# Attention's last loop: the diagonal square of scores computed as ten blocks and six TensorE transposes of finished exponentials

## The chip, the core and the metric

The kernel runs on one NeuronCore of a Trainium2 chip, in one launch. The engines are called as in the profile: PE (TensorE: matmuls and transposes; PEld is its weight load), DVE (VectorE), ACT (ScalarE), POOL (GpSimd) and SP (SyncE, which only issues DMAs). The metric is the device time of the whole kernel in microseconds, lower is better; a kernel's time is the median of its runs.

## The reference, cut to what matters

The input `x` is four images of 64 x 64 tokens with 128 channels. A first layer is a state-space block (three scans per image). A second layer is attention followed by a small feed-forward part and a mixture of experts. The change lies in the attention, which has 16 heads of 8 channels over the 4096 tokens of an image (the shape comes from `x`, not from the constants in the setup):

```python
heads = x.reshape(Bs, Ss, H, D)
qkv = _qz_ring(heads + rx_theta)            # cosines and running products
q = jnp.transpose(qkv, (0, 2, 1, 3))
scores = jnp.einsum('bhsd,bhtd->bhst', q, q) / np.sqrt(D)
attn = jax.nn.softmax(scores, axis=-1)
ctx = jnp.einsum('bhst,bhtd->bhsd', attn, q)
```

Queries, keys and values are the same tensor `q`. So the scores of token s with token t are those of t with s, and so are their exponentials: the matrix of exponentials is symmetric. The kernel doesn't subtract a maximum; it sums the exponentials through an extra column of ones in the values and divides afterwards.

## The kernel before

The program goes through the four images. A fill stage makes the inputs of the scans, then `Attention.loop` runs once per image (three times with the scans of the next image beside it, a fourth time alone with the closing work of the third and fourth images beside it), and an end stage finishes the last tokens and the experts. The fourth call, `block.loop(nb - 1, ...)`, is "the last loop" here.

**Turns and rounds.** A call of `loop` does 32 *turns*: four groups `j` of four heads by eight blocks `qb` of 512 queries. In the last loop they are sorted by query block (`by_block`), so that the tokens of a block are finished early and their closing work can run beside later turns. A turn has 32 *rounds*, one for each tile `kc` of 128 keys (`NT` is 32). Each round does three things for four heads `k`:

- `scores(i)`: four PE matmuls (line 998, `s<-qm,key`), each with 32 rows of one head's split keys (a high and a low part), giving keys on 128 partitions by 512 queries; two heads share one PSUM tile `s` of two banks (pool `ps_s`, three such tiles). Then ACT takes the exponential of each PSUM tile into an SBUF tile `e` of 1024 columns (line 1003; pool `exps`, four tiles).
- `values(i)`: four matmuls (line 1012, `acc<-e,val`) that multiply the four heads' exponentials with their values (32 columns of weights each) and add into four 32-partition strips of one PSUM tile `acc` (`ps_o`, one tile). In fp32 each matmul is two instructions, so the profile counts eight.
- `beside(i)`: a step or two of the closing work of other tokens, between the scores and the values in program order.

**What sets the order.** The stage is written under `tc.manual_schedule()`, so each engine runs its instructions in the order of the Python code. For round `i` this is: scores of round `i + 1`, then the work beside, then the values of round `i`. PE is thus one round of scores ahead. `sums` (line 1021) copies `acc` out on DVE in the last loop and leaves five POOL DMAs (lines 1027 and 1030) for three rounds later.

**Keys and queries.** Every fourth round `fetch` brings the chunk of 512 keys three chunks ahead (lines 968 and 980: `key<-d_q`, `val<-d_v`, SP's queue; ten buffers each). `masked` loads a turn's 512 queries twelve rounds ahead.

**The work beside.** `Pace.turn(share, free)` adds `share` to a credit each round and runs steps while there is credit; a step that begins with PE work only runs where `free` is true. Here the share is 1.5, and `free` is `i % 3 > 0 or i > 830`. The steps are lines 1098 to 1215: L1115 (`co`), L1138 (`zt`), L1156 (`h`), L1169 (`fo`), L1193 (`xT`), L1207 (`lg`) on PE, with small DVE steps after each; and L1342 and L1353 of the experts. In the end stage L1384, L1394 and L1407 are the experts' matmuls and transposes; L1394 are four 128x128 transposes, and L1407 are products on four strips of 32 partitions with 128 moving columns.

Of the kernel before, what the change touches and what calls it, by code (L numbers as in the profile page):

```python
# [11 lines left out]
F32 = mybir.dt.float32  # L12
AF = mybir.ActivationFunctionType
# [3 lines left out]
P = 128  # L17
C = 128
L = 4096
NT = L // P  # L20
# [11 lines left out]
H, D, FFN = 16, 8, 512  # L32
VW = 9
VJ = 60
QB = 512
F32R = mybir.dt.float32r
# [74 lines left out]
def turned(nc, a, turns, bias=None):  # L111


    if bias:
        nc.scalar.activation(turns, a, AF.Identity, scale=1.0 / (2.0 * math.pi), bias=bias[0])
        nc.scalar.activation(turns, turns, AF.Identity, bias=bias[1])
    else:
        nc.vector.tensor_scalar(turns, a, 1.0 / (2.0 * math.pi), ROUND, ALU.mult, ALU.add)
        nc.vector.tensor_scalar_sub(turns, turns, ROUND)
    nc.vector.scalar_tensor_tensor(a, turns, -TWO_PI_HI, a, ALU.mult, ALU.add)  # L120
    nc.vector.scalar_tensor_tensor(a, turns, -TWO_PI_LO, a, ALU.mult, ALU.add)
    if bias:
# [591 lines left out]
class Attention:  # L714
# [62 lines left out]
    def begin(self, loop):  # L777

        tc = self.tc
        self.pieces_of(loop, 2)  # L780
        self.big = loop.enter_context(tc.tile_pool(name="a_big", bufs=1))
        self.mid = loop.enter_context(tc.tile_pool(name="a_mid", bufs=2))
        self.exps = loop.enter_context(tc.tile_pool(name="a_exps", bufs=4))
        self.ps_s = loop.enter_context(tc.tile_pool(name="a_ps_s", bufs=3, space=PSUM))
        self.ps_o = loop.enter_context(tc.tile_pool(name="a_ps_o", bufs=1, space=PSUM))

# [158 lines left out]
            if x % 3 == 2:  # L945
                yield

    def loop(self, b, beside, by_block=False):
# [10 lines left out]
        rounds = [(j, qb, kc) for j, qb in turns for kc in range(NT)]  # L959
        queries, keys, weights, es, accs, later = {}, {}, {}, {}, {}, {}  # L960
        chunks = [(j, g) for j, _ in turns for g in range(NT // 4)]
        held = {}

        def halves(to, j, cut, first):


            src = self.q[b].rearrange("(k j) x d t -> j k (x d) t", j=4)[j]
            nc.sync.dma_start(out=to, in_=src[:, first * D : (first + 4) * D, cut])

        def fetch(at):  # L970

            if at >= len(chunks):
                return
            j, g = chunks[at]
            if held.get(g) != j:
                held[g] = j
                keys[g] = self.big.tile([P, QB], F32, tag="keys", bufs=10, name=f"key_{b}_{at}")
                halves(keys[g], j, slice(g * QB, (g + 1) * QB), 0)
                weights[g] = self.big.tile([P, 4, VJ], F32, tag="values", bufs=10, name=f"val_{b}_{at}")
                nc.sync.dma_start(out=weights[g], in_=self.v[b][:, j, g * 4 : g * 4 + 4, :])  # L980
            keys[f"{at}"], weights[f"{at}"] = keys[g], weights[g]

        def masked(j, qb):
            t = self.mid.tile([P, QB], F32, tag="qm", name=f"qm_{b}_{j}_{qb}")
            halves(t, j, slice(qb * QB, (qb + 1) * QB), 2)
            queries[j, qb] = t

        def scores(i):

            j, qb, kc = rounds[i]  # L990
            es[i] = []
            cut = slice(kc % 4 * P, kc % 4 * P + P)
            for pair in range(2):
                s_ps = self.ps_s.tile([P, 2, QB], F32, tag="s", name=f"s_{b}_{i}_{pair}")
                for k in range(2):
                    at = 32 * (2 * pair + k)
                    rows = slice(at, at + 32)
                    nc.tensor.matmul(  # L998
                        s_ps[:, k, :], keys[f"{i // 4}"][rows, cut].bitcast(F32R), queries[j, qb][rows, :].bitcast(F32R),
                        start=True, stop=True,  # L1000
                    )
                e = self.exps.tile([P, 2, QB], F32, tag="e", name=f"e_{b}_{i}_{pair}")
                nc.scalar.activation(e, s_ps, AF.Exp, scale=1.0 / math.sqrt(D))  # L1003
                es[i].append(e)

        def values(i):
            j, qb, kc = rounds[i]
            if kc == 0:
                accs[j, qb] = self.ps_o.tile([P, QB], F32, tag="acc", name=f"acc_{b}_{j}_{qb}")
            v = weights[f"{i // 4}"][:, kc % 4, :]  # L1010
            for k in range(4):
                nc.tensor.matmul(  # L1012
                    accs[j, qb][32 * k : 32 * k + 32, :], v[:, k * VW : k * VW + 32],
                    es[i][k // 2][:, k % 2, :], start=(kc == 0), stop=(kc == NT - 1),
                )
            del es[i]

        def sums(j, qb, i):

            av = self.mid.tile([P, QB], F32, tag="av", name=f"av_{b}_{j}_{qb}")  # L1020
            (nc.vector.tensor_copy if by_block else nc.scalar.copy)(av, accs.pop((j, qb)))  # L1021
            cut = slice(qb * QB, (qb + 1) * QB)

            def store():
                for k in range(4):
                    h = 4 * k + j
                    nc.gpsimd.dma_start(  # L1027
                        out=self.context[b][h * D : h * D + D, cut], in_=av[32 * k : 32 * k + D, :]
                    )
                nc.gpsimd.dma_start(  # L1030
                    out=self.total[b][qb].rearrange("(k j) t -> j k t", j=4)[j], in_=av[D::32, :]
                )
                if by_block and j == 3:
                    self.whole[b] = qb + 1

            later[i + 3] = store

        masked(0, 0)
        for at in range(3):
            fetch(at)  # L1040
        scores(0)
        for i, (j, qb, kc) in enumerate(rounds):
            if i % 4 == 0:
                fetch(i // 4 + 3)
            if i + 1 < len(rounds):
                scores(i + 1)
            if kc == NT - 12 and i + 12 < len(rounds):
                masked(*rounds[i + 12][:2])
            if i in later:
                later.pop(i)()  # L1050
            beside(i)
            values(i)
            if kc == NT - 1:
                sums(j, qb, i)
        for i in sorted(later):
            later[i]()
        self.whole[b] = L // QB
# [464 lines left out]
def tile_kernel(tc, ctx, x, in_proj_w, dirs, out_proj_w, attn, gate, weight1, weight2, out):  # L1522


    nc = tc.nc
    nb = x.shape[0]
# [30 lines left out]
    block = Attention(tc, ctx, attn, gate, cols, ident, bank, dram, t1, w_out, scans, inputs.sz, x)  # L1557
# [10 lines left out]
    block.bank = bank  # L1568
    loop = ExitStack()
    block.begin(loop)  # L1570
    scans.extra = loop.enter_context(tc.tile_pool(name="s_extra", bufs=1))
    with tc.manual_schedule():
        last = Pace()
        n = 3 * NC * NB
        for b in range(nb - 1):
# [24 lines left out]
            last = Pace(block.after(b))  # L1600
# [6 lines left out]
    blocks = L // QB  # L1607
    pairs = [(b, b + 1) for b in range(0, nb - 2, 2)] + [(nb - 2,), (nb - 1,)]
    with tc.manual_schedule():
        last = Pace(  # L1610
            last.parts, experts.biases(),
            *(
                part for images in pairs[:-1]
                for part in (experts.search(images, blocks), experts.choice(images, blocks), experts.gather(images))
            ),
            block.after(nb - 1, range(0, 4)), block.after(nb - 1, range(4, 6)), block.after(nb - 1, range(6, blocks - 1)),
            experts.search(pairs[-1], blocks - 1),
        )
        block.loop(nb - 1, lambda i: last.turn(1.5, i % 3 > 0 or i > 830), True)
        last.rest()  # L1620
        block.cut = False
    loop.close()
# [49 lines left out]
```

## Time and profile before

| | us |
|---|---|
| median of 3 runs (11411.24 to 11415.38) | 11413.67 |
| the profiled execution | 11412.32 |
| its span, first to last instruction | 11410.5 |
| last loop, 9126 to 11162 | 2036 |
| ACT busy in the last loop | 1925.4 |
| DVE busy in the last loop | 393.7 |
| L1003, exp of 128x1024 in the last loop, x2048 | 1904.7 |
| mean granted TensorE clock of the run, and in the last loop | 0.942, 0.98 |

How to read it: the span is the profiled execution's own, and 1.8 us lie around it. The busy time of an engine is the union of its instructions; matmuls are pipelined and their ends modelled, so a PE that looks busy isn't at its peak. A wait is put down to the semaphore that came last. In a timeline an ACT line with a start 0.92 us after the one before it is a back-to-back exponential: one of them lasts about 1.06 us, and the next starts before it is over.

### The profile page before, as it was taken

Reading aid. Unit: us, or ns where it says so; the run is one execution under the profiler, and the core shown is the slowest. Engines: PE = TensorE matmul, PEld = TensorE weight load, DVE = VectorE, ACT = ScalarE, POOL = GpSimd, SP = SyncE. Lnnn points to the kernel's source line nnn. Section 1 sums busy time; section 2 is a strip of 40 time slices with the busy share of each in tenths; the row PEclk is TensorE's granted clock in tenths of the full one; section 3 lists DMA queues with packets and bytes.
Section 4 is the critical chain, followed back from the end, with each engine's and each line's share of the span. In section 5 each row is a group of like instructions: output and inputs, shape, how many; then the busy total and the mean of one; then the engine's idle time right before and its main releaser. Section 6 shows DMA issues by size and latency. Waiting matters only on the chain.

```text
span 11410.5 us, 183033 instructions
## 1 busy us (share of the span) xinstructions
PE 9874.3 (87%) x68358; PEld 3273.6 (29%) x68358; DVE 8258.3 (72%) x8405; ACT 9993.7 (88%) x10828; POOL 3790.3 (33%) x3891
## 2 busy tenths in 40 slices
PE   6687792788998889899998899999998999999995
PEld 2233331222222222222222222222222223333323
DVE  6889997888888987999988979988998321111212
ACT  4566672899999999999999999999999999989992
POOL 4777784332323223424333124243331110000000
PEclk8798895899999999999999999999999999999997
DMA  6778897656565665665656755656556332222225
GB/s 188 226 231 230 226 249 198 161 145 156 142 155 155 178 174 146 158 154 142 151 147 160 194 157 156 156 141 151 146 147 162 116 100 72 76 71 84 75 65 186
DMA packets 900980, 1747.52 MB, mean 153 GB/s; under 512 B 203150, under 2 KB 443846, under 8 KB 899830
## 3 DMA queue, kind: packets, MB, share of 16 engines
q1 hardware_dynamic: 764734, 1469.68, 47.9%
q0 software_dynamic: 93856, 156.41, 4.8%
q10 hardware_dynamic: 41496, 109.71, 3.6%
q8 instruction: 537, 8.80, 0.3%
q14 instruction: 357, 2.92, 0.1%
HBM read 1379.76 MB, written 355.47 MB: 152 GB/s over the span
## 4 chain that ended last, share of the span: by engine, by line
PE 38%; ACT 24%; issue 14%; DVE 11%; DMA 10%; POOL 1%; SPq 1%; ACTq 0%; DVEq 0%; POOLq 0%
PE acc L1012 21%; ACT e L1003 20%; PE s L998 10%; DVE h L561 5%; DMA delta<-d_delta 4%; PE cv L412 2%; DMA du<-d_du 2%; DVE dB L551 1%; ACT dA L542 1%; PE y L599 1%; ACT delta L542 1%; PE fo L1169 1%; PE xd L426 1%; PE h L1156 1%; DMA w<-in_L_ffn_weight_dram 1%
## 5 line engine op out<-in xcount | busy, mean ns | idle before, releaser
L1003 ACT ACTIVATE e<-s 128x1024 f32<-128x1024 f32 x8192 | 7778.1, 1105 | 234.2 <-PE s L998 222.2
L1012 PE MATMUL acc<-e,val 128*32 128x512 f32 x32768 | 5250.2, 615 | 106.5 <-ACT av L1021 93.7
L998 PE MATMUL s<-qm,key 32*128 32x512 f32 x16384 | 2650.8, 501 | 588.8 <-ACT e L1003 558.9
L998 PEld LDWEIGHTS s<-qm,key 32*128 32x128 f32 x16384 | 1013.4, 184 | 4444.4 <-issue 2483.9
L563 POOL COPY ends<-h 128x1 f32<-128x1 f32 x1152 | 1333.8, 1159 | 2362.4 <-DVE h L561 2353.2
L551 DVE TENSOR_TENSOR dB<-du,B 128x1024 f32<-128x1024 f32 x960 | 1213.6, 1264 | 441.2 <-PE y L599 217.2
L1012 PEld LDWEIGHTS acc<-e,val 128*32 128x32 f32 x32768 | 973.5, 109 | 1608.4 <-issue 789.0
L561 DVE TENSOR_TENSOR_SCAN h<-dA,ends,dB 128x1024 f32<-128x1024 f32 x576 | 1351.2, 2346 | 110.3 <-ACT dA L542 66.2
L542 ACT ACTIVATE dA<-delta,A 128x1024 f32<-128x1024 f32 x768 | 935.7, 1218 | 500.5 <-DMA delta<-d_delta 460.8
L561 DVE TENSOR_TENSOR_SCAN h<-delta,ends,du 128x1024 f32<-128x1024 f32 x432 | 1013.2, 2345 | 127.2 <-ACT delta L542 64.3
L568 POOL TENSOR_TENSOR hC<-h,C 128x1024 f32<-128x1024 f32 x384 | 993.5, 2588 | 153.3 <-PE y L599 83.7
L542 ACT ACTIVATE delta<-delta,A 128x1024 f32<-128x1024 f32 x768 | 937.4, 1221 | 7.3 <-DVE dB L551 2.2
L572 DVE TENSOR_TENSOR du<-h,C 128x1024 f32<-128x1024 f32 x576 | 702.2, 1219 | 0.1
L572 DVE TENSOR_TENSOR dB<-h,C 128x1024 f32<-128x1024 f32 x576 | 702.2, 1219 | 0.0
L551 DVE TENSOR_TENSOR du<-du,B 128x1024 f32<-128x1024 f32 x576 | 691.6, 1201 | 5.8 <-DMA B<-d_bc 5.8
L1027 POOL DMA_DIRECT2D d_ctx<-av x512 | 260.3, 518 | 1026.1 <-DVE av L1021 647.6
L412 PE MATMUL cv<-xn,conv 128*128 128x512 f32 x1024 | 469.7, 612 | 26.8 <-DVE xn L346 17.2
L593 POOL DMA_DIRECT2D d_du<-x_delta x272 | 157.2, 578 | 1003.0 <-DVE x_delta L592 945.1
L561 DVE TENSOR_TENSOR_SCAN h<-dA,dB 128x1024 f32<-128x1024 f32 x192 | 438.9, 2286 | 50.3 <-ACT dA L542 40.9
L599 PE MATMUL y<-hC,sel 128*32 128x256 f32 x3072 | 247.8, 456 | 171.7 <-DVE o L615 160.0
L599 PE MATMUL y<-dB,sel 128*32 128x256 f32 x4608 | 378.8, 401 | 9.9 <-DVE xT L1196 4.8
L561 DVE TENSOR_TENSOR_SCAN h<-delta,du 128x1024 f32<-128x1024 f32 x144 | 329.1, 2285 | 68.3 <-issue 35.0
(246 smaller groups left out, 7200.5 us busy)
## 6 DMA issues: line engine op xcount, KB each, us to landing
delta<-d_delta SPq DMA_DIRECT2D x768, 512.0 KB
du<-d_du SPq DMA_DIRECT2D x576, 512.0 KB
du<-d_du ACTq DMA_DIRECT2D x192, 512.0 KB
key<-d_q SPq DMA_DIRECT2D x352, 256.0 KB
d_u<-u SPq DMA_DIRECT2D x48, 1024.0 KB
d_delta<-r SPq DMA_DIRECT2D x48, 1024.0 KB
B<-d_bc SPq DMA_DIRECT2D x96, 512.0 KB
C<-d_bc SPq DMA_DIRECT2D x96, 512.0 KB
```

What stands on the lines that cost most here:

```text
L412: nc.tensor.matmul(banks[2 * m + g], w["conv"][:, k, m * P : (m + 1) * P], reads(k, g), start=(k == 0), stop=(k == 3))
L542: nc.scalar.activation(tiles["delta", s], t, AF.Exp, scale=A)
L551: nc.vector.tensor_mul(tiles["du", s], du, spread[order, c, "B", j % 2])
L561: nc.vector.tensor_tensor_scan(h, dA, dB, first, ALU.mult, ALU.add)
L563: nc.gpsimd.tensor_copy(ends[order, c][:, at : at + 1], h[:, T - 1 :])
L568: nc.gpsimd.tensor_mul(tiles["du", s], h, spread[order, c, "C", j % 2])
L572: nc.vector.tensor_mul(dB, h, spread[order, c, "C", j % 2])
L599: nc.tensor.matmul(y[32 * g : 32 * g + 32, : T // 4], self.sel[:, j // 2, :], hC[:, 256 * g : 256 * g + 256], start=(j == 0), stop=(j == 3),)
L998: nc.tensor.matmul(s_ps[:, k, :], keys[f"{i // 4}"][rows, cut].bitcast(F32R), queries[j, qb][rows, :].bitcast(F32R), start=True, stop=True,)
L1003: nc.scalar.activation(e, s_ps, AF.Exp, scale=1.0 / math.sqrt(D))
L1012: nc.tensor.matmul(accs[j, qb][32 * k : 32 * k + 32, :], v[:, k * VW : k * VW + 32], es[i][k // 2][:, k % 2, :], start=(kc == 0), stop=(kc ...
L1027: nc.gpsimd.dma_start(out=self.context[b][h * D : h * D + D, cut], in_=av[32 * k : 32 * k + D, :])
```

## The change

In the last loop only (`mirror=True`), the 512 keys that are the same tokens as a turn's 512 queries are treated apart. That square has sixteen blocks of 128 by 128 per head. Of these the ten on and above the diagonal are computed and exponentiated as before; the other six are transposes of finished blocks:

- The own chunk comes first in a turn and gives three rounds for four: *top* (key tile 0, all 512 queries), *odd* (key tile 1 with queries 128 to 511, and key tile 3 with queries 384 to 511, side by side in one tile of 512) and *even* (key tile 2 with queries 256 to 511, half a tile). Top is the turn's first round, odd its eleventh, even its twenty-first; a turn has 31 rounds.
- After the values of such a round, `turned` transposes the blocks right of the diagonal on PE (four per block, one per head) into a PSUM tile from the pool of the scores, and DVE copies them to an SBUF tile `m` (one buffer). Top turns blocks (0,1) and (0,2) at once and (0,3) in the next round, so its exponentials are kept longer; odd turns (1,2) and (1,3); even turns (2,3).
- One round later, right after the next scores and ahead of the work beside, `added` multiplies each turned block with the values of its key tile into 128 columns of `acc` (four matmuls per block).
- The pool of exponentials has five tiles for four, `av` one buffer for two. The share of the work beside is 1.55, and PE steps are free after round 804.

The diff, cut to its core (renamed indices, which leave the other loops as they were, are left out):

```diff
-        self.exps = loop.enter_context(tc.tile_pool(name="a_exps", bufs=4))
+        self.exps = loop.enter_context(tc.tile_pool(name="a_exps", bufs=5))
...
+        for j, qb in turns:
+            order = [qb] + [g for g in range(NT // 4) if g != qb] if mirror else range(NT // 4)
+            base = len(chunks)
+            chunks += [(j, g) for g in order]
+            turn = [(j, qb, base + x // 4, x % 4) for x in range(NT)]
+            if mirror:
+                own, turn = [(j, qb, base, kind) for kind in ("top", "odd", "even")], turn[4:]
+                turn = own[:1] + turn[:9] + own[1:2] + turn[9:18] + own[2:] + turn[18:]
+            rounds += turn
...
                 for k in range(2):
+                    if kind == "odd":
+                        product(s_ps[:, k, :384], at, 1, 2 * pair + k, slice(128, 512))
+                        product(s_ps[:, k, 384:], at, 3, 2 * pair + k, slice(384, 512))
+                    elif kind == "even":
+                        product(s_ps[:, k, :256], at, 2, 2 * pair + k, slice(256, 512))
+                    else:
+                        product(s_ps[:, k, :], at, 0 if kind == "top" else kind, 2 * pair + k, slice(0, 512))
...
+                wide = slice(0, 256 if kind == "even" else 512)
+                nc.scalar.activation(e[:, :, wide], s_ps[:, :, wide], AF.Exp, scale=1.0 / math.sqrt(D))
...
         def values(i):
...
+            if kind == "top":
+                turned(i, [(0, 1), (0, 2)])
+                mirrors.append((i, [(0, 3)]))
+            elif kind == "odd":
+                turned(i, [(1, 2), (1, 3)])
+            elif kind == "even":
+                turned(i, [(2, 3)])
...
+        def turned(i, blocks):
+            j, qb, at, _ = rounds[i]
+            n = len(blocks)
+            ps = self.ps_s.tile([P, 2, QB], F32, tag="s", name=f"t_{b}_{i}_{blocks[0][1]}")
+            for x, (r, c) in enumerate(blocks):
+                for k in range(4):
+                    nc.tensor.transpose(ps[:, x, k * P : k * P + P], block_of(i, r, c, k), self.ident)
+            m = self.mid.tile([P, 2, 4, P], F32, tag="mirror", bufs=1, name=f"m_{b}_{i}_{blocks[0][1]}")
+            nc.vector.tensor_copy(m[:, :n].rearrange("p x k t -> p x (k t)"), ps[:, :n])
+
+            def added():
+                for x, (r, c) in enumerate(blocks):
+                    for k in range(4):
+                        add(j, qb, at, c, k, slice(r * P, r * P + P), m[:, x, k, :])
+
+            waiting.append(added)
...
             if i + 1 < len(rounds):
                 scores(i + 1)
...
+            while waiting:
+                waiting.pop()()
+            for of, blocks in mirrors:
+                turned(of, blocks)
+                del es[of]
+            mirrors.clear()
             beside(i)
             values(i)
...
-        block.loop(nb - 1, lambda i: last.turn(1.5, i % 3 > 0 or i > 830), True)
+        block.loop(nb - 1, lambda i: last.turn(1.55, i % 3 > 0 or i > 804), True, True)
```

More of the change, by code (lines that the diff above doesn't have):

```diff
@@ L946, in rings, with loop @@
                 yield
-    def loop(self, b, beside, by_block=False):
+    def loop(self, b, beside, by_block=False, mirror=False):
         nc = self.nc
@@ L958, in loop @@
             turns.sort(key=lambda turn: turn[1])
-        rounds = [(j, qb, kc) for j, qb in turns for kc in range(NT)]
         queries, keys, weights, es, accs, later = {}, {}, {}, {}, {}, {}
-        chunks = [(j, g) for j, _ in turns for g in range(NT // 4)]
-        held = {}
+        rounds, chunks, held, mirrors = [], [], {}, []
+        for j, qb in turns:
[7 more added lines that the diff above has]
+            rounds += turn
+        per = len(rounds) // len(turns)
         def halves(to, j, cut, first):
@@ L986, in masked, with product @@
             queries[j, qb] = t
+        def product(to, at, kind, k, cut):
+            rows = slice(32 * k, 32 * k + 32)
+            key = keys[f"{at}"][rows, kind * P : kind * P + P]
+            nc.tensor.matmul(
+                to, key.bitcast(F32R), queries[rounds[self.at][:2]][rows, cut].bitcast(F32R), start=True, stop=True,
+            )
         def scores(i):
-            j, qb, kc = rounds[i]
-            es[i] = []
-            cut = slice(kc % 4 * P, kc % 4 * P + P)
+            j, qb, at, kind = rounds[i]
+            self.at, es[i] = i, []
             for pair in range(2):
@@ L995, in scores @@
                 for k in range(2):
[L996 to L1001, printed above, removed]
+                    if kind == "odd":
[5 more added lines that the diff above has]
+                        product(s_ps[:, k, :], at, 0 if kind == "top" else kind, 2 * pair + k, slice(0, 512))
@@ L1002, in scores, with add @@
                 e = self.exps.tile([P, 2, QB], F32, tag="e", name=f"e_{b}_{i}_{pair}")
-                nc.scalar.activation(e, s_ps, AF.Exp, scale=1.0 / math.sqrt(D))
+                wide = slice(0, 256 if kind == "even" else 512)
+                nc.scalar.activation(e[:, :, wide], s_ps[:, :, wide], AF.Exp, scale=1.0 / math.sqrt(D))
                 es[i].append(e)
+        def add(j, qb, at, kc, k, cut, e, start=False, stop=False):
+            v = weights[f"{at}"][:, kc, :]
+            nc.tensor.matmul(
+                accs[j, qb][32 * k : 32 * k + 32, cut], v[:, k * VW : k * VW + 32], e, start=start, stop=stop,
+            )
@@ L1006, in values @@
         def values(i):
-            j, qb, kc = rounds[i]
-            if kc == 0:
+            j, qb, at, kind = rounds[i]
+            if i % per == 0:
                 accs[j, qb] = self.ps_o.tile([P, QB], F32, tag="acc", name=f"acc_{b}_{j}_{qb}")
-            v = weights[f"{i // 4}"][:, kc % 4, :]
             for k in range(4):
[L1012 to L1015, printed above, removed]
@@ L1016, in values @@
-            del es[i]
+                if kind == "even":
+                    add(j, qb, at, 2, k, slice(256, 512), es[i][k // 2][:, k % 2, :256])
+                elif kind == "odd":
+                    add(j, qb, at, 1, k, slice(128, 512), es[i][k // 2][:, k % 2, :384])
+                else:
+                    kc = 0 if kind == "top" else kind
+                    add(j, qb, at, kc, k, slice(0, 512), es[i][k // 2][:, k % 2, :], i % per == 0, i % per == per - 1)
+            if kind == "odd":
+                for k in range(4):
+                    add(j, qb, at, 3, k, slice(384, 512), es[i][k // 2][:, k % 2, 384:])
@@ new lines, in values, with block_of @@
+            if kind == "top":
+                turned(i, [(0, 1), (0, 2)])
+                mirrors.append((i, [(0, 3)]))
+            elif kind == "odd":
+                turned(i, [(1, 2), (1, 3)])
+            elif kind == "even":
+                turned(i, [(2, 3)])
+            if i not in (m[0] for m in mirrors):
+                del es[i]
+        def block_of(i, r, c, k):
+            return es[i][k // 2][:, k % 2, (c - r) * P : (c - r) * P + P]
+        def turned(i, blocks):
[9 more added lines that the diff above has]
+                for x, (r, c) in enumerate(blocks):
+                    for k in range(4):
+                        add(j, qb, at, c, k, slice(r * P, r * P + P), m[:, x, k, :])
+            waiting.append(added)
@@ L1018, in sums @@
+        waiting = []
         def sums(j, qb, i):
-            av = self.mid.tile([P, QB], F32, tag="av", name=f"av_{b}_{j}_{qb}")
+            av = self.mid.tile([P, QB], F32, tag="av", bufs=1, name=f"av_{b}_{j}_{qb}")
             (nc.vector.tensor_copy if by_block else nc.scalar.copy)(av, accs.pop((j, qb)))
@@ L1036, in sums @@
             later[i + 3] = store
-        masked(0, 0)
+        masked(*turns[0])
         for at in range(3):
@@ L1041, in loop @@
         scores(0)
-        for i, (j, qb, kc) in enumerate(rounds):
-            if i % 4 == 0:
-                fetch(i // 4 + 3)
+        seen = -1
+        for i, (j, qb, at, kind) in enumerate(rounds):
+            if at > seen:
+                seen = at
+                fetch(at + 3)
             if i + 1 < len(rounds):
                 scores(i + 1)
-            if kc == NT - 12 and i + 12 < len(rounds):
+            if i % per == per - 12 and i + 12 < len(rounds):
                 masked(*rounds[i + 12][:2])
@@ L1050, in loop @@
                 later.pop(i)()
+            while waiting:
[4 more added lines that the diff above has]
+            mirrors.clear()
             beside(i)
             values(i)
-            if kc == NT - 1:
+            if i % per == per - 1:
                 sums(j, qb, i)
```

## The prediction

> **What bounds the kernel now.** I read the stages first, then who waits for whom in the last loop, then single rounds. The change touches the last loop alone, from 9126 us (the last copy of the loop before it, L1021 on ACT) to 11162 us. Stages; after the stage come length, then busy us (xinstructions) of PE, PEld, DVE, ACT and POOL, then clock:
>
> ```profile
> core 0: us, PE busy (x) PEld busy (x) DVE busy (x) ACT busy (x) POOL busy (x), PEclk, DMA share, GB/s
> 9126.00:11162.00 2036.00, 1964.26 (x13696) 631.71 (x13692) 393.68 (x996) 1925.36 (x2079) 177.06 (x314) 0.98 0.26 76
> 9400.00:9800.00 400.00, 397.27 (x429) 1.00 0.23 69
> ```
>
> The second row is L1003 (exp) alone: 429 exps in 400 us where little else runs. So ACT holds the loop, and PE looks as full only because its overlapping ends are modelled. DVE has 1642 us free. The waits of the same stretch (total us, times, longest):
>
> ```profile
> PEld acc L1012 <- ACT e L1003: 123.1, 424, 0.8
> ACT e L1003 <- PE s L998: 99.1, 82, 7.5
> PEld acc L1012 <- DVE av L1021: 19.7, 25, 3.5
> ```
>
> The two engines wait for each other: PE for an exp 424 times, ACT for scores 82 times. One undisturbed round from the timeline (start, duration):
>
> ```profile
> 9932.37 1.11 ACT L1003 ACTIVATE e<-s 128x1024 f32<-128x1024 f32 x1
> 9932.69 0.51 PE L998 MATMUL s<-qm,key 32*128 32x512 f32 x4
> 9933.13 0.14 PEld L1012 LDWEIGHTS acc<-e,val 128*32 128x32 f32 x4 [0.25 <-issue]
> 9933.29 1.12 ACT L1003 ACTIVATE e<-s 128x1024 f32<-128x1024 f32 x1
> 9933.54 0.14 PEld L1012 LDWEIGHTS acc<-e,val 128*32 128x32 f32 x4 [0.27 <-ACT e L1003]
> 9934.52 0.51 PE L998 MATMUL s<-qm,key 32*128 32x512 f32 x4
> 9935.12 2.03 ACT L1003 ACTIVATE e<-s 128x1024 f32<-128x1024 f32 x2
> ```
>
> Scores 9932.69 to 9933.13 (0.43 us); the first two heads' values; then the other two wait until the exp of 9932.37 is done (9933.54); they end at 9934.52, where the next scores start. The round is 1.83 us. Those scores are used 0.60 us later by the exp of 9935.12, exactly when ACT is ready. Where four L1169 matmuls stood ahead of the values, scores started at 9902.95 and their exp at 9903.54, again 0.6 us, after ACT had waited. So the order is tight: PE can take in some 0.40 us between scores and values (values without a wait take 0.99, here 1.40), and whatever comes **after** the values delays ACT at once. ACT's delay is never made good, since it has no faster pace than 0.915 us an exp.
>
> **What the Trainium skill says.** *ScalarE: Activation LUTs*, section "What ACT_TABLE_LOAD costs": an ACTIVATE with immediate scale costs 186 ns + 0.833 ns an element, neighbours overlapping by 93 ns. For 1024 that is 1039; the loop's mean is 1061 and its spacing 915, so the trace agrees. For 512 elements I estimate a spacing of 0.915 - 0.427 = 0.49 us. *TensorEngine Tiling (Array Packing)*, "Key Properties": changing the tiling mode drains the engine. Transposes (128x128) lie between values (128x32) and scores (32x128), so they change it twice; the rows below contain such changes. *VectorE: DVE Perf Modes*, "Why PSUM operands drop a tier": fp32 from PSUM goes at one element a cycle. The trace agrees (0.266 us for 256 more, below). *TensorE: Matmul & The Clock Gate*, Part 2, step 1: matmuls stay in program order. So a matmul that waits for DVE holds all behind it; the third wait row above shows one.
>
> **The change, part by part**, for one of 32 turns. Prices (PE from start to the next start):
>
> ```profile
> 9929.46 0.44 PE L1193 MATMUL xT<-ident,x1r 128*128 128x128 f32 x2
> 9929.83 1.10 PE L1012 MATMUL acc<-e,val 128*32 128x512 f32 x8
> ...
> 11294.29 0.66 PE L1394 MATMUL hT<-ident,hr 128*128 128x128 f32 x4 [0.76 <-ACT hr L1389]
> 11294.88 1.06 PE L1384 MATMUL h<-w,pooled 128*32 128x512 f32 x8
> ...
> 11299.64 1.08 PE L1407 MATMUL o<-w,hs 128*32 128x128 f32 x32 [1.51 <-ACT hs L1402]
> 11300.54 1.04 PE L1384 MATMUL h<-w,pooled 128*32 128x512 f32 x8
> ```
> ```profile
> 9935.44 0.69 DVE L1196 COPY xT<-xT 128x512 f32<-128x512 f32 x1
> L1348 DVE COPY wT<-wt 128x256 f32<-128x256 f32 x24 | 10.2, 425 | 83.1 <-PE wt L1342 83.1
> ```
>
> Two transposes 0.37, four 0.59, so 0.11 each past the first: eight cost 1.03. L1407 has the very form of the mirrored products (four column groups, 128 columns, two instructions each): 0.90/32 = 28 ns, so 16 instructions cost 0.45 and 8 cost 0.22. Copies: 512 columns 0.69; 1024 columns 0.69 + 2 x 0.266 = 1.22.
>
> *Removed:* a turn has 31 rounds for 32, -1.83 us. Two of its exps are half as wide.
>
> *Top round* (blocks 1 and 2 turned after its values, block 3 one round later). Time 0 is the start of the next round's scores; undisturbed, later scores start at 1.83, 3.66, 5.49. Values end at 1.83, eight transposes take them to 2.86: scores 1.03 late. They end at 3.29. The mirrored products stand next in PE's order and wait for DVE: the last transpose ends 0.07 after the next start and DVE starts 0.11 later (as L1394 and its reader do), so 2.86 + 0.18 + 1.22 + 0.05 = 4.31. PE stands 1.02 us; behind it are block 3's transposes, the next values and scores, and for those ACT. Products to 4.76, four transposes to 5.35, values 0.99 to 6.34: the second scores are 6.34 - 3.66 = **2.68 late**. The order of the built program shows that second pair waiting for block 3's copy: 5.35 + 0.18 + 0.69 + 0.05 = 6.27, in time. The last 8 products (0.22) then fit: scores at 7.98 + 0.60 = 8.58, ACT is ready at 8.78.
>
> *Odd round* (two blocks): the same without block 3: 4.76 + 0.99 = 5.75, **2.09 late**. Its scores are eight matmuls, two after each other on one row group, 512 columns together; no row has that. Between 0 (full overlap) and 0.7 (none, 1.1 for 0.43); I take **0.30**.
>
> *Even round* (one block): the round before it ends with its own wait, so the two short exps (0.49 each) gain nothing. Its values take 0.49, four transposes 0.59: scores could start at 0.43 + 0.49 + 0.59 = 1.51, but the turned block has taken one of three score buffers, so the second pair waits for the next round's second exp: 0.60 + 0.92 + 1.11 = 2.63. Then 0.43, products 0.22, values 0.99: 4.27 for 3.66, **0.61 late**.
>
> Sum: 2.68 + 2.09 + 0.30 + 0.61 - 1.83 = +3.85 us a turn, x32 = **+123 us**. This holds where ACT bounds. Where the work beside makes PE bound, PE's own sum counts: transposes 2 x 1.03 + 2 x 0.59 = 3.24, products 1.35, two waits 2.04, less 1.5 rounds' values 1.49 and scores 0.65, plus 0.5 for the odd scores: +5.0 us, x32 = 160. The copies also queue behind other DVE work: the 25 waits for av took 19.7 us where 0.69 + 0.1 - 0.43 = 0.36 each would be 9, so some 0.25 us more; two exposed copies a turn: +16 us. I take 123 + 16 = 139.
>
> At nothing: the extra DVE time (4 copies, 3.8 us a turn, into 51 us free), the longer life of the first key chunk (its buffer of ten is not refilled until after the last use), one av buffer for two (stores end three rounds on), a fifth exp buffer. That buffer doesn't free ACT: no ACT wait for values is in the list. The pace 1.55 x 992 rounds gives 1538 steps, 1.5 x 1024 gave 1536, so the work beside ends with the loop as before; if not, its rest runs bare behind it. No DMA is added.
>
> **Sum.** Profiled execution 11412.3 us (span 11410.5 plus 1.8; median of the runs 1.4 higher) + 139 = **11551 us**.
>
> **The rivals.** (B) *Faster:* the turning hides and only the exps saved show. 32 x (2 whole exps x 0.915 + 2 x 0.427) = 86 us, giving 11326. For it: ACT is 94.6% busy in the loop and DVE mostly idle. It decides once the four disturbances cost under 1.83 us a turn in all, for which PE would need slack after values; the 0.60 us hand-over speaks against it. (C) *DVE's queue:* copies stand behind DVE instructions that wait for a DMA or for POOL (longest wait for av 3.5 us). With 1.5 us more on 64 exposed copies: 11551 + 96 = 11647. (D) Disturbances of half the size, 2.84 - 1.83 = 1.0 a turn: +32 us, 11445; and if a little less, no change.
>
> **How the numbers follow.** 0.2% is 23 us, about what a measurement of this kernel can tell from no change. Forecast 72%, own range 11490 to 11625 (odd scores 0 to 0.7: -10 to +13; PE-bound throughout +37; copies never waited for, 2 x 1.02 x 32: -65). B 14%; C 10%; D 4%, counted as same. So faster 0.14, same 0.04, slower 0.82. The range 11440 to 11650 takes in the forecast and most of C and D and leaves out B.
>
> **What would show it.** The last loop lasts 2175 us for 2036; exps of it 1920 whole and 64 half-wide; a new wait of PE for the mirror's copy, about 1 us, 64 times or more; ACT's wait for scores up from 99 us to some 300; eight transposes near 1.03, 16 products near 0.45. Wrong if that wait is short, or if scores after a turning start as before.

## The result and the profile after

| | us |
|---|---|
| after, median of 4 runs (11537.13 to 11555.27) | 11543.56 |
| before, median of 4 runs (11411.24 to 11422.50) | 11414.52 |
| ratio, 95% interval | 1.0113 (1.0096 to 1.0131) |
| after, the profiled execution (the longest of the four), and its span | 11555.27, 11553.6 |

The change makes the kernel 129 us slower by the medians; the two profiled executions, read below, lie 143 us apart. In the code of after, scores are line 999, exponentials L1019, values and mirrored products both L1024 (told apart by `acc<-e` and `acc<-m`), transposes L1062 and their copies L1064.

The last loop and the rest behind it, busy time by stage as in the table of before:

```profile
9121.00:11307.00 2186.00, 2045.92 (x16004) 749.20 (x16000) 512.97 (x1124) 1857.12 (x2015) 177.90 (x314) 0.97 0.24 71
11307.00:11553.00 246.00, 120.94 (x1156) 90.10 (x1156) 73.78 (x154) 30.61 (x49) 25.78 (x47) 0.67 0.63 216
```

The loop grew from 2036 to about 2185 us, and everything else stayed (246 us behind it; 248.5 before). ACT's busy time fell by 68 us in a loop 149 us longer: ACT now has 329 us free where it had 111. The groups of the loop, each form by itself (count, then busy us and mean ns, then idle of the engine ahead of them):

```profile
L1019 ACT ACTIVATE e<-s 128x1024 f32<-128x1024 f32 x1917 | 1801.8, 1047 | 324.4 <-PE s L999 287.4 <-PE t L1062 29.5
L1019 ACT ACTIVATE e<-s 128x512 f32<-128x512 f32 x64 | 36.4, 652 | 1.7 <-PE s L999 1.7
L1064 DVE COPY m<-t 128x1024 f32<-128x1024 f32 x64 | 78.3, 1223 | 276.8 <-PE t L1062 276.7
L1064 DVE COPY m<-t 128x512 f32<-128x512 f32 x64 | 44.2, 691 | 182.7 <-PE t L1062 182.7
```

And who waits for whom (total us, times, longest):

```profile
ACT e L1019 <- PE s L999: 289.1, 260, 9.0
PE acc L1024 <- DVE m L1064: 72.6, 68, 6.9
PEld acc L1024 <- ACT e L1019: 91.9, 309, 0.8
```

ACT's wait for scores went from 99 to 289 us, and there is a new wait of PE for the mirror's copy: 72.6 us in 68, 52 of them of 0.88 or 0.89 us. PE waits for exponentials less often (309 times for 424), since it now comes late by itself. The DVE instructions that were added cost 122 us, but DVE is idle for three quarters of the loop; only their latency counts. One top round with little work beside it, on PE:

```profile
9465.17 0.51 PE L999 MATMUL s<-qm,key 32*128 32x512 f32 x4
9465.50 0.59 PE L1221 MATMUL h<-zT,w 8*128 8x256 f32 x2
9466.05 1.07 PE L1024 MATMUL acc<-e,val 128*32 128x512 f32 x8
9467.05 1.09 PE L1062 MATMUL t<-ident,e 128*128 128x128 f32 x8
9468.07 0.51 PE L999 MATMUL s<-qm,key 32*128 32x512 f32 x4
9469.46 0.65 PE L1024 MATMUL acc<-m,val 128*32 128x128 f32 x16 [0.88 <-DVE m L1064]
9470.03 0.66 PE L1062 MATMUL t<-ident,e 128*128 128x128 f32 x4
9470.62 1.07 PE L1024 MATMUL acc<-e,val 128*32 128x512 f32 x8
9471.62 0.51 PE L999 MATMUL s<-qm,key 32*128 32x512 f32 x4
```

Eight transposes take 1.02 us (9467.05 to 9468.07). Scores end 0.43 after that, at 9468.50, and PE then stands until 9469.46, 0.96 us, for the copy; it takes 0.57 for 16 products, 0.59 for four transposes, 1.00 for values. From the scores of 9465.17 to those of 9471.62 it is 6.45 us where three undisturbed rounds less one are 3.66: 2.79 late. ACT shows the same three delays (start, length, idle before):

```profile
9449.10 18.68 ACT L1019 ACTIVATE e<-s 128x1024 f32<-128x1024 f32 x20 [1.24 <-PE s L999]
9468.67 1.02 ACT L1019 ACTIVATE e<-s 128x1024 f32<-128x1024 f32 x1 [0.90 <-PE s L999]
9470.57 1.03 ACT L1019 ACTIVATE e<-s 128x1024 f32<-128x1024 f32 x1 [0.87 <-PE t L1062]
9472.22 3.77 ACT L1019 ACTIVATE e<-s 128x1024 f32<-128x1024 f32 x4 [0.62 <-PE s L999]
```

Back-to-back exponentials overlap by about 0.13 us here, so each idle time is that much more of delay; counted from start to start, less the usual 0.915, the three are 1.03 + 0.99 + 0.74 = 2.76 us. The exponential of 9470.57 is put down to the transposes "t": it writes into the tile that top's exponentials hold for their third block. That adds nothing: it is over before 9471.62, when the scores of the next exponential (9472.22) only start. The last two delays are one wait for these scores, cut in two.

### The profile page after: what moved, and what is told of

It reads as the page before. It is cut to its first block, busy times and chain, and to the rows that moved or that the text cites. A ratio compares the mean times of both kernels' runs of the same rounds, so it can differ in the third digit from the quotient of the medians.

```text
span 11553.6 us, 187418 instructions
## 1 busy us (share of the span) xinstructions
PE 9957.7 (86%) x70662; PEld 3388.9 (29%) x70662; DVE 8380.8 (73%) x8533; ACT 9925.0 (86%) x10764; POOL 3759.2 (33%) x3891
## 4 chain that ended last, share of the span: by engine, by line
PE 36%; ACT 25%; issue 14%; DVE 14%; DMA 10%; SPq 1%; POOL 1%; ACTq 0%; DVEq 0%; POOLq 0%
ACT e L1019 21%; PE acc L1024 20%; PE s L999 9%; DVE h L561 6%; DMA delta<-d_delta 4%; PE cv L412 2%; DVE dB L551 2%; DMA du<-d_du 2%; ACT delta L542 1%; ACT dA L542 1%; PE t L1062 1%; PE fo L1234 1%; DVE m L1064 1%; PE y L599 1%; PE h L1221 1%
## 5 line engine op out<-in xcount | busy, mean ns | idle before, releaser
L1019 ACT ACTIVATE e<-s 128x1024 f32<-128x1024 f32 (+1 forms) x8128 | 7709.8, 1099 | 453.0 <-PE s L999 387.9
L1024 PE MATMUL acc<-e,val 128*32 128x512 f32 x32768 | 5156.3, 611 | 104.2 <-ACT av L1078 94.6
L563 POOL COPY ends<-h 128x1 f32<-128x1 f32 x1152 | 1298.8, 1128 | 2376.1 <-DVE h L561 2355.3
L1024 PEld LDWEIGHTS acc<-e,val 128*32 128x32 f32 x32768 | 961.6, 109 | 1558.2 <-issue 769.1
L1064 DVE COPY m<-t 128x1024 f32<-128x1024 f32 (+1 forms) x128 | 122.5, 957 | 459.5 <-PE t L1062 459.4
```

The lines of the kernel that those rows point to most:

```text
L563: nc.gpsimd.tensor_copy(ends[order, c][:, at : at + 1], h[:, T - 1 :])
L1019: nc.scalar.activation(e[:, :, wide], s_ps[:, :, wide], AF.Exp, scale=1.0 / math.sqrt(D))
L1024: nc.tensor.matmul(accs[j, qb][32 * k : 32 * k + 32, cut], v[:, k * VW : k * VW + 32], e, start=start, stop=stop,)
```

## The experiments

All ratios are to the kernel before, measured together with each run, with their 95% interval; "cost" is the difference of the two medians.

**e1_buffers.** Kernel before, with the diff's loop code but no turning, and the buffers that it uses:

```diff
-        self.exps = loop.enter_context(tc.tile_pool(name="a_exps", bufs=4))
+        self.exps = loop.enter_context(tc.tile_pool(name="a_exps", bufs=5))
...
-                keys[g] = self.big.tile([P, QB], F32, tag="keys", bufs=10, name=f"key_{b}_{at}")
+                keys[g] = self.big.tile([P, QB], F32, tag="keys", bufs=9, name=f"key_{b}_{at}")
...
-            av = self.mid.tile([P, QB], F32, tag="av", name=f"av_{b}_{j}_{qb}")
+            av = self.mid.tile([P, QB], F32, tag="av", bufs=1, name=f"av_{b}_{j}_{qb}")
```

> The kernel before with only the edits around the turning: five exponential tiles for four, one av buffer for two, and nine key and value buffers for ten (which e4 needs), no turning, the old pace. Theory (all of the loss comes from what the turning puts behind values and ahead of values on PE): 11414, within 10 us of before. Rival (the tighter or larger buffers cost something themselves): over 11425.

Measured: 11407.92 us for 11407.14, ratio 1.0000 (0.9992 to 1.0008). The values' tiles also have nine buffers for ten. All these buffers together cost nothing that shows; the interval is some 9 us to either side.

**e2_ten_blocks.** The six turned blocks are left out; the three own rounds stay.

```diff
-            if kind == "top":
-                turned(i, [(0, 1), (0, 2)])
...
-                turned(i, [(2, 3)])
```

> The changed kernel without transposes, copies and mirrored products: it leaves out six of the sixteen blocks of each own square, so only the saving is left. Theory (PE and ACT are bound to each other round by round, so that a half-wide exp round saves nothing): 32 x 1.83 = 59 us less than before, 11356. Rival (ACT's own time counts, whole exps and halves): 86 us less, 11328. The odd scores cost 0 by the trace of the changed kernel; if they cost the forecast 0.30 it is 11365.

Measured: 11350.40, ratio 0.9949 (0.9936 to 0.9961): 57 us saved (44 to 73 by the interval), 1.8 us a turn. This is one round's 1.83 us and nothing for the two half-wide exponentials of a turn, though these are short (652 ns for 1047). The trace shows where their gain goes:

```profile
9361.77 3.77 ACT L1019 ACTIVATE e<-s 128x1024 f32<-128x1024 f32 x4 [0.65 <-PE s L999]
```

The two half-wide exponentials before this line start at 9359.93 and 9360.41, 0.48 us apart, and then ACT stands for the next scores; the two together take 1.84 us from start to next start, as long as two whole ones. So all that turning can ever gain in this order of work is 57 us, not the 86 us of an ACT-only count, and the turning itself costs some 129 + 57 = 186 us.

**e3_no_products.** Transposes and copies stay, the mirrored products are left out (the line `waiting.append(added)`).

> Transposes and DVE copies stay, the mirrored products (and so PE's wait for the copies) are left out: six of sixteen blocks are missing from the sums. Theory, by the same walk: top 1.03 + 0.19, odd 1.03, even 0.39, less 1.83, so +0.8 a turn, +26 us on before: 11440. Rival 1 (the transposes and the score buffer that they take are the whole cost): 11543 as the changed kernel. Rival 2 (the products' wait for DVE is the whole cost): 11356 as without any turning.

**e4_a_round_later.** The products come one round later, with a mirror tile for each size, so that DVE has a round's time to copy.

```diff
-            waiting.append(added)
+            waiting.append([2, added])
...
-            while waiting:
-                waiting.pop()()
+            for entry in list(waiting):
+                entry[0] -= 1
+                if entry[0] == 0:
+                    waiting.remove(entry)
+                    entry[1]()
```

> The whole computation, each mirrored product one round later than in the changed kernel (a second mirror tile; nine key and value buffers), so that DVE's copy is done when PE comes to it. Theory: the two waits of 0.96 us go and the products fit into PE's slack of 0.40 but for 0.05 to 0.2: top 1.17, odd 1.08, even 0.4, less 1.83, +0.8 a turn: 11441. Rival 1 (transposes and score buffers are the whole cost): 11543. Rival 2 (the wait is the whole cost): under 11400, faster than before.

Measured: e3 11467.30, ratio 1.0054 (1.0041 to 1.0066), cost 60; e4 11501.49, ratio 1.0081 (1.0069 to 1.0094), cost 94. Both missed the theory, e3 by 34 us and e4 by some 67, and lie between it and rival 1; rival 2 is out. Where the wait went is in e4's list of waits:

```profile
PE t L1062 <- DVE m L1064: 26.4, 30, 0.9
PE s L999 <- DVE m L1064: 7.7, 4, 2.5
```

e3 has 26.3 us in 30 and 7.4 us in 4 in the same rows. The third block of a top round goes, one round after the first two, into a PSUM tile of the scores' pool of three; the other two hold the next scores, so it waits for the tile that DVE is still copying out. The same copy is waited for, 30 times, with or without a product behind it. All of PE's waits for the mirror's copies come to 74 us in after and to 38 us in e4; these 36 us are what e4 gained on after (129 - 94 = 35). The theory was right in that the wait for DVE is dear, and wrong in that the product alone is what waits.

**e5_four_blocks.** No third block: key tile 3 with query blocks 0 and 2 goes into the idle half of the even round, so that twelve blocks are computed in three whole rounds and four turned.

```diff
                     elif kind == "even":
                         product(s_ps[:, k, :256], at, 2, 2 * pair + k, slice(256, 512))
+                        product(s_ps[:, k, 256:384], at, 3, 2 * pair + k, slice(0, 128))
+                        product(s_ps[:, k, 384:], at, 3, 2 * pair + k, slice(256, 384))
...
-                mirrors.append((i, [(0, 3)]))
...
-                turned(i, [(2, 3)])
```

> The whole computation with twelve blocks computed in three full rounds (the even round also takes key tile 3 with queries 0 to 127 and 256 to 383) and four turned: top turns (0,1) and (0,2), odd (1,2) and (1,3), nothing else. Everything else as changed. Theory (a turning of two blocks costs the 2.0 us that the odd round shows in the changed kernel, and the third block of top and the even round's turning come on top of that): 2 x 2.0 - 1.83 = 2.2 a turn, 11407 + 70 = 11477. Rival (the cost goes with the number of blocks, 186 us over e2 for six, 31 each): 11350 + 124 = 11474 as well, so this run mainly gives the base for the next; but a cost of the even round other than its turning would show as over 11490.

**e6_four_later.** e5 with the products a round later, by the edit of e4.

> As e5, with the mirrored products one round later, so that they don't wait for the copy. In e4 the third block of top waited for the copy of the first two in place of the products, since it needs the same score buffer; here there is no third block. Theory (PE's wait for the copy is a real loss of 0.96 us, 64 times): 61 us under e5, near 11416. Rival (waits for the copy are covered, as the small gain of e4 suggests: 35 us for six blocks): some 20 us under e5, near 11455.

Measured: e5 11484.14, ratio 1.0067 (1.0055 to 1.0080), cost 74; e6 11434.39, ratio 1.0018 (1.0011 to 1.0025), cost 24. e5 came near both of its numbers (11477 and 11474), which it could not tell apart. From e5 to e6, PE's waits for the copies fall from 64 to 7 us, and 50 us come back (61 by the theory's 0.96 x 64, 20 by the rival): that is what the two exposed copies of a turn cost. With the wait gone, the products fit into PE's slack. The rest of e6 is in its ACT timeline, around a top round:

```profile
9394.82 18.83 ACT L1021 ACTIVATE e<-s 128x1024 f32<-128x1024 f32 x20 [0.84 <-PE s L999]
9414.48 31.34 ACT L1021 ACTIVATE e<-s 128x1024 f32<-128x1024 f32 x33 [0.83 <-PE s L999]
```

One delay per turning is left where after had two or three, 0.84 + 0.13 = 0.97 us: the eight transposes after the values. Two of them are 1.94 us a turn against the 1.83 saved, so e6 can at best break even. It does so in its last turn, which has no work beside (58.73 us, before 58.85); its 24 us lie where work stands beside (the fifteenth turn takes 82.4 us in e6, 77.3 in e2 and 73.9 in before).

**e7_own_bank.** The transposes leave the place after the values, and the scores' pool. One block at a time goes into the PSUM bank that the work beside uses, between scores and values, where PE has some 0.4 us to wait anyway.

```diff
-            ps = self.ps_s.tile([P, 2, QB], F32, tag="s", name=f"t_{b}_{i}_{blocks[0][1]}")
+            ps = self.bank.grab(f"t_{b}_{i}_{blocks[0][1]}")
...
+            self.bank.leave()
...
+            if waiting:
+                waiting.pop(0)()
+            elif mirrors and self.bank.free:
+                of, left = mirrors[0]
+                turned(of, [left.pop(0)])
             beside(i)
```

> Four turned blocks, one at a time, into the PSUM bank of the work beside whenever it is free, between scores and values, with the product a round or more later; six exponential tiles, one mirror tile of half the size, nine key and value buffers. Nothing then stands between values and scores, and no score buffer is taken. Theory (PE has 0.40 us of slack there; four transposes take 0.59, a product 0.23): 4 x 0.19 - 1.83 = -1.07 a turn, 11407 - 34 = 11373, faster than before. Rival (PE has no slack left beside the other work, so each PE instruction counts wherever it stands: 4 x 0.82 - 1.83 = +1.45): 11453.

**e8_idle_rounds.** e7 with the turning only in rounds without PE work beside (`i % 3 == 0`), or after six rounds.

> As e7, with blocks turned in the rounds in which the work beside may not begin PE steps, or when a block has waited for over six rounds. Theory: the same sum with fewer rounds that hold both, 11365 to 11373. Rival: blocks wait longer, exponential tiles are held and ACT waits for them, over 11385.

Measured: e7 11486.19, ratio 1.0063 (1.0050 to 1.0075), cost 76; e8 11505.08, ratio 1.0085 (1.0071 to 1.0098), cost 95. Both missed the theory with the wrong sign. e7 lies above its rival's 11453 too; for e8 the rival (over 11385) held. PE in a round of e7:

```profile
9405.13 0.66 PE L1065 MATMUL t<-ident,e 128*128 128x128 f32 x4
9406.57 0.71 PE L1240 MATMUL fo<-w,h 128*128 128x128 f32 x4 [0.78 <-DVE m L1067]
9407.21 1.07 PE L1026 MATMUL acc<-e,val 128*32 128x512 f32 x8
```

The bank counts as free for the program as soon as the copy is issued; so the work beside takes it in the same round, and its matmuls (`fo`) stand 0.78 us for DVE's copy with the values behind them. A wait was taken out of one place and put into another by the buffer that was borrowed: all of PE's waits for the mirror's copies come to 70 us in e7, and to 74 in after.

That the place itself is right shows in e7's last turn, in which no work stands beside. From the end of one turn's sums to the end of the next (DVE's copies of `acc`), before and then e7:

```profile
11103.05 0.69 DVE L1021 COPY av<-acc 128x512 f32<-128x512 f32 x1 [58.15 <-PE acc L1012]
11161.90 0.69 DVE L1021 COPY av<-acc 128x512 f32<-128x512 f32 x1 [58.16 <-PE acc L1012]
```
```profile
11166.00 0.69 DVE L1082 COPY av<-acc 128x512 f32<-128x512 f32 x1 [17.82 <-PE acc L1026]
11223.03 0.69 DVE L1082 COPY av<-acc 128x512 f32<-128x512 f32 x1 [31.36 <-PE acc L1026]
```

This turn takes 57.03 us in e7 with its four blocks turned, 58.85 in before, and 56.74 in e2, which turns nothing. Here turning in PE's slack is all but free. Over the whole loop e7 is 2.3 us a turn slower than before, so the loss comes with the work beside. This is one turn of one execution, but the last turns of e8 and e11, also without work beside, take 57.07 and 57.05 us.

e8 was slower than e7 by 19 us, and its trace has what its rival named: ACT waits 28 us in 16 times for a tile of exponentials that PE's values or transposes still hold, where e7 has no such wait over 0.15 us.

**e9_bank_kept.** e7, the bank given back only after the work beside has had its turn in that round.

```diff
             beside(i)
+            if kept:
+                self.bank.leave()
             values(i)
```

> As e7, but the bank is given back only after the work beside has had its step, so that the work beside doesn't take it in the same round and stand on PE until DVE has emptied it (e7 showed PE's fo and h matmuls waiting 0.8 us for the mirror's copy, ahead of the values). Theory (that wait was what e7 lost; a block between scores and values costs 0.19 us): quiet turns 4 x 0.19 - 1.83 = -1.07 against before, 11410 - 34 = 11376, up to 11395 with the turns in which the work beside fills PE's slack. Rival (PE has no slack beside the other work, or the work beside falls behind without its bank and runs on after the loop): over 11410.

**e10_kept_idle.** The same edit of e8.

> As e9, with blocks turned in rounds in which the work beside may not begin PE steps, or when a block has waited for over six rounds. Theory: 11370 to 11385, a little under e9, since fewer rounds hold both. Rival: the exponential tiles are held longer and ACT waits for them as in e8, which was 19 us over e7.

Measured: e9 11456.76, ratio 1.0041 (1.0029 to 1.0054), cost 48; e10 11432.18, ratio 1.0020 (1.0011 to 1.0028), cost 23. Both missed the theory. For e9 the rival held, in its second half; e10 is under e9, as its theory said, and the wait for held tiles that its rival named is 8 us. The loop and the rest behind it, e9:

```profile
9126.00:11139.00 2013.00, 1945.56 (x15897) 700.29 (x15896) 441.51 (x1023) 1873.58 (x2015) 165.92 (x295) 0.98 0.25 75
11139.00:11460.70 321.70, 157.38 (x1271) 113.89 (x1269) 110.68 (x255) 29.64 (x49) 37.02 (x66) 0.64 0.53 177
```

This loop is 23 us shorter than before's, but it also holds less work, so it doesn't show a saving. Where the bank is held, the work beside skips its turn; 115 more PE instructions are left behind the loop (1271 for 1156), where they run bare, and the rest lasts 322 us for 248.5.

**e11_quick_pace** and **e12_idle_quick.** e9 and e10 with a quicker pace, so that the work beside ends with the loop:

```diff
-        block.loop(nb - 1, lambda i: last.turn(1.55, i % 3 > 0 or i > 804), True, True)
+        block.loop(nb - 1, lambda i: last.turn(1.9, i % 3 > 0 or i > 620), True, True)
```

(e12: 1.7 and 780.)

> Four blocks turned, each alone in the bank of the work beside, which is given back only after that work's turn (e9_bank_kept), with a faster pace for the work beside (1.9 instead of 1.55 a round, all rounds from 620 on), so that it ends with the loop. Theory: e9 lost to the kernel before only by its tail (322 us after the loop for 249), while its loop was 23 us shorter; with the tail back at 249 to 260 the kernel takes 11390 to 11410 us, ratio 0.998 to 1.000. Rival: the loaded rounds have no room left on PE, so work moved back into the loop lengthens it by what the tail saves: 11420 to 11450.

> The same with the turnings in the rounds without work beside (e10_kept_idle), pace 1.7 and all rounds from 780 on. e10's loop ended 4 us before that of the kernel before and its tail was 24 us longer. Theory: with the tail back, 11405 to 11415 us, ratio 1.000. Rival: 11425 to 11445, the work moved back lengthens the loop by what the tail saves.

Measured: e11 11447.22, ratio 1.0038 (1.0025 to 1.0052), cost 41; e12 11462.53, ratio 1.0050 (1.0037 to 1.0063), cost 56. For e11 the rival held; e12 came out above even its rival's 11445. e11:

```profile
9126.00:11200.00 2074.00, 1971.31 (x15928) 710.22 (x15928) 475.85 (x1122) 1869.55 (x2004) 174.51 (x309) 0.96 0.25 74
11200.00:11447.70 247.70, 122.70 (x1158) 91.71 (x1156) 74.35 (x154) 30.59 (x49) 25.76 (x47) 0.68 0.62 214
```

The rest is back at 248 us, and the loop has grown by 61 us of the 74 that the rest gave up. The work beside and the turning draw on the same slack of PE, and it doesn't hold both. No version beat the kernel before.

## Why the prediction was right, point by point

It said 11551 us, and 11543.56 was measured. The mechanism held; that the sum came within 8 us is in part luck, since one term was too large and the work beside was left out. Its terms, in us for a turn, against places of the traces where little work stands beside:

| term | predicted | measured |
|---|---|---|
| top round | 2.68 | 2.76 (ACT's three delays above) |
| odd round with its scores | 2.09 + 0.30 | 1.97 (ACT's delays at 9426.17 and 9428.98) |
| even round | 0.61 | 0.57 (after; four exponentials from 9572.88 to 9577.11, less 3.66) |
| one round fewer | -1.83 | -1.77 (e2: 56.7 / 32) |
| sum | 3.85 | 3.53 |
| copies behind other DVE work | 0.50 | 0.4 (see below) |
| work beside | 0 | see below |
| all, mean of a turn | 4.35 | 4.64 (148.6 / 32, loop of the profiled execution) |

- *PE can't take more after the values, and ACT's delay is never made good.* Right: e6's single delay after each turning, and the 289 us that ACT waits.
- *PE stands for the mirror's copy, 1.02 us.* Right: 0.96 in the top round shown, and 50 us back when this was taken away (e5 to e6). In the last turn, without work beside, it is 60.69 us for e5 and 58.73 for e6: 0.98 for each of the two copies. The 0.06 between 1.02 and 0.96 is DVE's start, 0.11 us after PE's next start (9468.07 to 9468.18) where the sum had 0.18. The rule of the Trainium skill that this step rested on, *TensorE: Matmul & The Clock Gate*, Part 2, step 1 (matmuls stay in program order), shows again in e7: values behind `fo`, `fo` behind a copy.
- *Prices.* Eight transposes 1.02 for 1.03, four 0.59 for 0.59, copies 1.22 and 0.69 as worked out, 16 products 0.57 after a wait for 0.45. One reading was loose: the figures that the prediction quotes from the Trainium skill, *ScalarE: Activation LUTs*, "What ACT_TABLE_LOAD costs", give exponentials a spacing of 1039 - 93 = 946 ns, and the trace has 915, so neighbours overlap by 146 ns of 1061; the measurement decides, and it is what the sum used.
- *Two matmuls in sequence on one row group cost 0.30.* Mis-sized: nothing. The eight matmuls of an odd round's scores start at 9420.87 and the values after them at 9421.32, 0.45 us later, where four take 0.43. This took 10 us too much into the sum.
- *The copies queue behind other DVE work, 16 us.* About right, though not by its own working: (19.7 - 9) / 25 is 0.43 us a wait, not 0.25, and would have given 27 us. Of PE's 68 waits, 8 are over 1 us (the longest 6.9) because the copy starts late on DVE; all 72.6 us less 0.88 for each leave 13 us, 0.4 a turn.
- *The work beside.* This is what the sum lacked. The last turn has none of it, and there after is 3.05 us slower than before (61.90 for 58.85), somewhat less than the 3.85 of the sum. The mean of all turns is 4.64, so 1.6 us a turn, 51 us, come with the work beside, 13 of them by the queue on DVE. A top round with four `fo` matmuls in it has 0.85 + 0.87 + 1.07 of ACT's idle time (from 9404.59 on) where the one shown has 2.39. The prediction worked out "+5.0 a turn" for where PE is bound, and gave it no weight in the sum. The last turn is one turn of one execution; how the other 38 us divide was not measured.
- *Half-wide exponentials gain nothing.* Right, by e2: this is where rival B failed, with 86 us for the most that could be gained, and 57 measured. Its deciding point (four disturbances under 1.83 us in all) was missed by 3.5.
- *Nothing else costs.* Right for the buffers (e1) and the rest behind the loop (246 us for 248.5). The new order of the chunks and the quicker pace are in e2 as well, where the whole round saved comes out.
- Rival C (1.5 us more on 64 copies) would need PE's waits at 2.5 us; their mean is 1.07. Rival D (half the disturbance) has the size of e6, but e6 turns four blocks; with six, and the products a round later, 94 us are left (e4).

What the prediction didn't see: the third block's transposes need the very PSUM tile that the first copy reads. In after this is hidden behind the products' wait for the same copy; it came out only where that wait was removed (e3, e4).

The parts of the turning cover each other, so the 186 us don't divide into costs of each part alone: taking the products out gives 69 back, moving them a round later 35 (six blocks) or 50 (four). The last turn, without work beside, has it at its cleanest (us, one turn of each profiled execution):

| last turn | us | less before |
|---|---|---|
| before | 58.85 | |
| e2, nothing turned | 56.74 | -2.11 |
| e3, six turned, no products | 60.11 | +1.26 |
| e4, products a round later | 60.15 | +1.30 |
| after | 61.90 | +3.05 |
| e5, four turned | 60.69 | +1.84 |
| e6, products a round later | 58.73 | -0.12 |
| e7, turned in PE's slack | 57.03 | -1.82 |

Products a round later add 0.04 us here (e3 to e4): they fit into PE's slack.

## What to carry to other kernels

Where PE and ACT hand work to each other with no slack, as here, removed work on ACT paid only by whole rounds (e2), and work added on PE between values and scores cost its full time (e6); count the disturbances per round saved. A step that goes PE, DVE, PE cost its latency on PE (0.96 us) unless a round lay between, and every buffer on the way (here a PSUM tile of the scores) was free without that same copy. Slack that a quiet stretch shows may be what the work beside lives on: the stretch where both meet decides, as e7 with its last turn, and e11, show.

## What the runs showed of the hardware that I had not expected

Two score matmuls of 384 and 128 columns after each other on one row group cost no more than one of 512: 0.45 us for eight against 0.43 for four. An exponential of half the columns lasts 652 ns for 1047, so 0.62 of the time; from start to next start it is 0.48 us for 0.915.
